# A deformable convolution's sampling loop on one core: a second PSUM buffer for transposed pixels, earlier stores, and other places for scratch data

## The chip, the core and the metric

The kernel runs on one core of a Trainium2 chip. A core has five engines that run side by side and wait for each other on semaphores: TensorE (PE, matrix products, whose results go to PSUM, eight banks[...]), VectorE (DVE), ScalarE (ACT), GpSimd (POOL) and SyncE (SP), which here only issues DMA transfers. The metric is the time of one execution on the device, in microseconds (us). The program's names, which the profile uses, tell which buffer an instruction writes and reads: `pq<-s,xt` is written from `s` and `xt`.

## What is computed

Eight images of 128 channels and 64 x 64 pixels go through two layers. The first is group normalisation, then a deformable 3 x 3 convolution, batch normalisation, ReLU and the residual sum. The second is group normalisation and a mixture of two of four 3 x 3 convolutions with a shared one. The change concerns the deformable convolution:

```python
om = conv(x, off_w) + off_b                       # 3 x 3, 27 channels of offsets and masks
off = om[:, :18].reshape(B, 9, 2, H, W)
mask = sigmoid(om[:, 18:])
py = off[:, :, 0] + (row - 1) + ky                # where each of 9 taps samples, for each pixel
px = off[:, :, 1] + (column - 1) + kx
# val: x at (py, px), bilinear between four pixels, 0 outside the image
val = val * mask
y = einsum('bckhw,ock->bohw', val, w) + b
```

## The kernel before

Bilinear weights are written as "tents": the weight of pixel row r for a sample at py is relu(1 - |py - r|). For each image five tents in y (times the mask) and five in x are made from the offsets, stored to two tables in DRAM, and loaded again, spread over partitions, as `y_wts` and `x_wts`. An image is 11 bands of 6 rows; a band is 11 tiles of 6 x 6 pixels. For each tile VectorE multiplies x and y weights into `s`, TensorE multiplies `s` with the tile's transposed pixels `xt` into `pq`, and ScalarE copies `pq` into `samples`. A band later TensorE convolves the samples into `py`, and ScalarE copies `py` into `y`. The tables of the next image are made beside the bands of this one, in small steps (a `yield` ends a step; `pause(n)` is n of them). The pools and buffers:

```python
ps_s = ctx.enter_context(tc.tile_pool(name="ps_s", bufs=1, space=PSUM))   # for the whole kernel
...                                                                        # in dense(), the first layer:
ps_c = st.enter_context(tc.tile_pool(name="ps_c", bufs=2, space=PSUM))
ps_q = st.enter_context(tc.tile_pool(name="ps_q", bufs=3, space=PSUM))
ps_y = st.enter_context(tc.tile_pool(name="ps_y", bufs=1, space=PSUM))
ps_t = st.enter_context(tc.tile_pool(name="ps_t", bufs=1, space=PSUM))
...
combos = [a1.tile([P, H // 2, W], F32, name=f"combo{i}") for i in range(2)]
tent_y = combos[0].rearrange("p h w -> p (h w)")[0:WB, 0:YSTEP]            # YSTEP is 594
x_wts = [a1.tile([P, NT1, T, T, TAPS], F32, name=f"xwts{i}") for i in range(3)]
y_wts = [a1.tile([P, T, 3, WB, 3], F32, name=f"ywts{i}") for i in range(2)]
samples = [a1.tile([P, T + 2, 3, 3, WB], F32, name=f"samples{i}") for i in range(2)]
```

A pool with n `bufs` hands out n buffers in turn: the instruction that writes the n+1st tile waits until the first has been read. The transposes of a band's pixels, four or three tiles to one PSUM buffer:

```python
def pixels(g):
    xts[g] = a2.tile([P, NT1, P], F32, name="xt")
    for c0 in range(0, NT1, 4):
        n = min(4, NT1 - c0)
        pt = ps_t.tile([P, 4, P], F32, name="pt")
        for c in range(n):
            nc.tensor.transpose(pt[0:QQ, c], picked[g % 2][:, c0 + c]..., ident)
            if c % 2 or c == n - 1:
                yield
        nc.scalar.copy(xts[g][0:QQ, c0 : c0 + n], pt[0:QQ, 0:n])
        yield
        yield
```

The loop over bands issues, for tile c of band g, in this order:

```python
weights(n + AHEAD)                       # VectorE: s, three tiles ahead
sample(n)                                # PE: pq; ScalarE: samples <- pq
load_x(g + 2, ...) or load_y(g + 2, ...) # GpSimd issues the weights of the band after next
next(ended, None)                        # ScalarE: y <- py of the band before, then its statistics and store
if g and c > 1:
    conv(g - 1, c - 2, py)               # PE: py, nine products per band
next(turned, None)                       # PE: transposes of band g + 1; ScalarE: xt <- pt
next(made, None)                         # a step of the next image's tables (normalising, offsets, tents)
if c == 5: pick(g + 2)                   # ScalarE: gathers pixels
```

The tents. For images after the first, each in one of two buffers, stored one step after the next was made:

```python
for i in range(NR):                      # NR is 5
    distance_x(i, every)                 # ScalarE: work[1][i % 2] = |offset + step|
    yield from distance_y(i)             # VectorE
    tent_x(i, every)                     # ScalarE: relu(1 - work)
    yield
    tent_y_of(i)                         # VectorE: work[0][i % 2]
    if i:
        store_y(i - 1)
        store_x(i - 1)
    yield from pause(2)
store_y(NR - 1)
store_x(NR - 1)
```

For the first image nothing runs beside the tables yet. Its y tents lie in the memory of `samples[0]` and its x tents in that of `samples[1]`; the x tents of the first three bands are made early, the rest late:

```python
early, rest = slice(0, FIRST * T), slice(FIRST * T, WB)
for i in range(NR):
    distance_x(i, early); tent_x(i, early)            # ScalarE, in samples[1]
for i in range(NR):
    ... y tents on VectorE, store_y(i); after i == 1 the early x tents are stored; then loads of band 0
pick(0); pixels(0)
for i in range(2):
    distance_x(i, rest); tent_x(i, rest)              # ScalarE, in samples[1]
for r in range(T):
    load_y(0, r, nc.gpsimd if r < 4 else nc.scalar)
pick(1)
for i in range(2, NR):
    distance_x(i, rest); tent_x(i, rest)
for t in (x_wts[1], x_wts[2], y_wts[1]):
    nc.vector.memset(t, 0.0)
for r in range(T):
    load_y(1, r, nc.gpsimd)
for q in range(Q):
    load_x(1, q, nc.sync)
for i in range(NR):
    nc.sync.dma_start(out=<table of x>, in_=<late x tents i>)
```

Of the kernel before, what the change touches and what calls it, by code (L numbers as in the profile page):

```python
# [8 lines left out]
F32 = mybir.dt.float32  # L9
# [7 lines left out]
P = 128  # L17
# [40 lines left out]
def deform_moe_conv(  # L58
# [23 lines left out]
    dram = ctx.enter_context(tc.tile_pool(name="dram", bufs=1, space=DRAM))  # L82
    ps_s = ctx.enter_context(tc.tile_pool(name="ps_s", bufs=1, space=PSUM))

# [27 lines left out]

    def group_affine(stats, scale=None, shift=None):

        mv = small.tile([P, 2], F32, name="mv")
        nc.vector.bn_aggr(mv, stats)
        pm = ps_s.tile([P, 4], F32, name="pm", tag="pss")
        nc.tensor.matmul(pm[:, 0:1], lhsT=gsel, rhs=mv[:, 0:1], start=True, stop=True)
        d = small.tile([P, 1], F32, name="d")
        nc.vector.tensor_tensor(d, mv[:, 0:1], pm[:, 0:1], ALU.subtract)  # L120
        e = small.tile([P, 1], F32, name="e")
        nc.vector.scalar_tensor_tensor(e, d, d, mv[:, 1:2], ALU.mult, ALU.add)
        pv = ps_s.tile([P, 4], F32, name="pv", tag="pss")
        nc.tensor.matmul(pv[:, 0:1], lhsT=gsel, rhs=e, start=True, stop=True)

        gm = small.tile([P, 1], F32, name="gm")
        nc.vector.tensor_tensor(gm, mv[:, 0:1], d, ALU.subtract)
        if scale is None:
            scale = small.tile([P, 1], F32, name="scale")
            shift = small.tile([P, 1], F32, name="shift")  # L130
        rsqrt(scale, pv[:, 0:1], GN_EPS)
        nc.vector.scalar_tensor_tensor(shift, gm, -1.0, scale, ALU.mult, ALU.mult)
        pooled = small.tile([P, 1], F32, name="pooled")
        nc.vector.tensor_tensor(pooled, d, scale, ALU.mult)
        return scale, shift, pooled
# [33 lines left out]
    def dense():  # L169

        with ExitStack() as st:
# [7 lines left out]
            ps_y = st.enter_context(tc.tile_pool(name="ps_y", bufs=1, space=PSUM))  # L179
            ps_t = st.enter_context(tc.tile_pool(name="ps_t", bufs=1, space=PSUM))  # L180

# [59 lines left out]
            def tables(b):  # L241
# [4 lines left out]
                def pause(n):  # L246
                    for _ in range(n):
                        yield
# [23 lines left out]
                yield from pause(3)  # L272
                pm = ps_s.tile([P, 4], F32, name="pm", tag="pss")
                nc.tensor.matmul(pm[:, 0:1], lhsT=gsel, rhs=mv[:, 0:1], start=True, stop=True)
# [7 lines left out]
                yield from pause(2)  # L282
                pv = ps_s.tile([P, 4], F32, name="pv", tag="pss")
                nc.tensor.matmul(pv[:, 0:1], lhsT=gsel, rhs=ev, start=True, stop=True)
# [49 lines left out]
                def tap(j, kx):  # L334

                    if kx == 1:
                        pcs[j] = ps_c.tile([P, CH], F32, name="pc")
                    lo, hi = max(0, 1 - kx), min(W, W + 1 - kx)
                    for q in range(4):
                        nc.tensor.matmul(  # L340
                            pcs[j][32 * q : 32 * q + 32].rearrange("p (h w) -> p h w", w=W)[
                                :, :, lo:hi
                            ],
                            lhsT=weight_of[j][:, kx],
                            rhs=combo_of[j][:, 8 * q : 8 * q + 8, lo + kx - 1 : hi + kx - 1],
                            start=(kx == 1), stop=(kx == 2),
                            skip_group_check=True,
                        )
# [45 lines left out]
                for j in range(4):  # L394
# [9 lines left out]
                    most[:, b : b + 1], omr, AX.X, ALU.max, apply_absolute_value=True  # L404
                )
                yield from pause(9)
                for k in range(3):
# [21 lines left out]
                if b:  # L429
                    work = a1.tile([WB, 2, 2, YSTEP], F32, name="work", tag="om")  # L430
                    tents = [[work[:, a, i % 2] for i in range(NR)] for a in range(2)]
                else:
                    tents = []
                    for t in samples:
                        flat = t.rearrange("p r y x w -> p (r y x w)")
                        tents.append(
                            [flat[0:WB, i * YSTEP : (i + 1) * YSTEP] for i in range(NR)]
                        )
                one = off_x[:, ROWPAD:]
# [26 lines left out]

                def distance_x(i, bases):
                    nc.scalar.activation(
                        tents[1][i].rearrange("p (w y x) -> p x y w", y=3, x=3)[..., bases],
                        by_bases[..., bases], AF.Abs, bias=steps[0:WB, i : i + 1],  # L470
                    )

                def tent_x(i, bases):
                    one = tents[1][i][:, TAPS * bases.start : TAPS * bases.stop]
                    nc.scalar.activation(one, one, AF.Relu, bias=1.0, scale=-1.0)
# [20 lines left out]
                if b:  # L496
                    every = slice(0, WB)
                    for i in range(NR):
                        distance_x(i, every)
                        yield from distance_y(i)  # L500
                        tent_x(i, every)
                        yield
                        tent_y_of(i)
                        if i:
                            store_y(i - 1)
                            store_x(i - 1)
                        yield from pause(2)
                    store_y(NR - 1)
                    store_x(NR - 1)
                    return  # L510
# [3 lines left out]
                for i in range(NR):  # L514
                    distance_x(i, early)
                    tent_x(i, early)
                for i in range(NR):
# [4 lines left out]
                    if i == 1:  # L522
                        for n in range(FIRST):
                            one = tents[1][0][:, n * XSTEP : n * XSTEP + 1]
                            nc.sync.dma_start(
                                out=bass.AP(
                                    tensor=x_table[b].tensor,
                                    offset=x_table[b].offset + (n * NR + NR - 1) * XSTEP,
                                    ap=[[HROW, WB], [HROW - XSTEP, NR], [1, XSTEP]],
                                ),  # L530
                                in_=bass.AP(
                                    tensor=one.tensor, offset=one.offset,
                                    ap=[list(one.ap[0]), [YSTEP, NR], [1, XSTEP]],
                                ),
                            )
# [8 lines left out]
                for i in range(2):  # L544
                    distance_x(i, rest)
                    tent_x(i, rest)
                for r in range(T):
                    load_y(0, r, nc.gpsimd if r < 4 else nc.scalar)
                pick(1)
                for i in range(2, NR):  # L550
                    distance_x(i, rest)
                    tent_x(i, rest)

                for t in (x_wts[1], x_wts[2], y_wts[1]):
                    nc.vector.memset(t, 0.0)
                for r in range(T):
# [3 lines left out]
                for i in range(NR):  # L560
# [6 lines left out]
                        ),  # L567
                        in_=tents[1][i][:, FIRST * XSTEP :].rearrange("p (n k) -> p n k", k=XSTEP),
                    )
# [162 lines left out]
            def reach():  # L732

                near = a1.tile([P, B], F32, name="near")
                nc.vector.tensor_scalar(near, most, float(REACH), None, ALU.is_lt)
                pn = ps_s.tile([P, B], F32, name="pn", tag="pss")
                nc.tensor.matmul(pn[0:1], lhsT=ones_r, rhs=near, start=True, stop=True)
# [77 lines left out]
    def general():  # L815

        with ExitStack() as st:
# [3 lines left out]
            ap4 = st.enter_context(tc.tile_pool(name="ap4", bufs=4))  # L821
            gdram = st.enter_context(tc.tile_pool(name="gdram", bufs=1, space=DRAM))
            ps_o = st.enter_context(tc.tile_pool(name="ps_o", bufs=1, space=PSUM))
            ps_x = st.enter_context(tc.tile_pool(name="ps_x", bufs=1, space=PSUM))
# [57 lines left out]
            def prepare(b, made):  # L882
# [6 lines left out]
                for c in range(NCH):  # L889
                    nc.vector.bn_stats(stats[:, c, :], pad[:, 1 + 8 * c : 9 + 8 * c, 1 : W + 1])  # L890
                scale, shift, _ = group_affine(stats)
                for c in range(NCH):
# [137 lines left out]
    def layer1():  # L1030
# [6 lines left out]
        with ExitStack() as st:  # L1037
            st.enter_context(tc.manual_schedule())
            b1 = st.enter_context(tc.tile_pool(name="b1", bufs=1))
            b2 = st.enter_context(tc.tile_pool(name="b2", bufs=2))  # L1040
            ps_m = st.enter_context(tc.tile_pool(name="ps_m", bufs=7, space=PSUM))
            NG = 4
# [320 lines left out]
```

## Time and profile before

| | |
|---|---|
| time, median of 3 runs | 1690.58 us (1688.41 to 1694.52) |
| span of the profiled execution | 1692.0 us |
| granted TensorE clock, mean | 0.972 of full speed |
| PE busy | 1580.2 us (93%) |
| DVE busy | 1094.8 us (65%) |
| ACT busy | 906.6 us (54%) |
| POOL busy | 955.5 us (56%) |
| moved by DMA | 235.83 MB, mean 139 GB/s |
| first product of a band (`pq`) starts | 68.29 us |
| last copy of `py` to `y` starts | 1306.48 us |

A busy share is an average over stages that have different limits. So the table is read together with the page's 40 slices and with tables by stage: a wait is worth what it costs in its own stage, on the engine that is full there. A matmul here is recorded as two passes, so "x2" of a product is one matmul; the ends of matmuls are modelled, and the starts are the better measure. A wait for several semaphores is put down to the one that came last by the profile.

### The profile page before, as it was taken

The page shows a single profiled execution, that of the slowest core. Times are in us where ns is not written, and L with a number is a line of the kernel's source. Part 1 is how long each engine was busy: PE and PEld are TensorE (multiplying, and loading weights), DVE is VectorE, ACT ScalarE, POOL GpSimd, SP SyncE. Part 2 cuts the span into 40 slices and gives each one's busy share as a digit, 9 for nine tenths or more (in the row PEclk, how much of TensorE's full clock was granted, in tenths as well). Part 3 has the DMA queues.
Part 4 walks back from the last instruction along what each step waited for, and adds up shares of the span by engine and source line. Part 5 has one row for each costly group of instructions (what it writes and reads, how often), then busy time and mean ns, then how long its engine had stood idle before and what let it go on. Part 6 is the DMA issues. An engine that isn't in the chain of part 4 may idle for free. (4 is left out here: it accounts for less than half of the span.)

```text
span 1692.0 us, 21036 instructions
## 1 busy us (share of the span) xinstructions
PE 1580.2 (93%) x6106; PEld 918.2 (54%) x6106; DVE 1094.8 (65%) x2151; ACT 906.6 (54%) x2096; POOL 955.5 (56%) x1518
## 2 busy tenths in 40 slices
PE   3399999999999999999999999999998479999998
PEld 1265665666566556656665665566665234444443
DVE  5755666567575746665665667465443888888882
ACT  2555764766576557647665765576654423333320
POOL 3375685669567666856685676677761412222210
PEclk9589999999999999999999999999999789999999
DMA  4644874776477467647754775665761624443211
GB/s 134 134 120 109 173 173 106 148 181 140 110 164 179 112 130 182 159 104 151 189 132 108 164 184 119 133 161 139 176 147 49 268 95 152 155 153 147 82 58 56
DMA packets 195671, 235.83 MB, mean 139 GB/s; under 512 B 131766, under 2 KB 146098, under 8 KB 195550
## 3 DMA queue, kind: packets, MB, share of 16 engines
q0 software_dynamic: 94768, 124.63, 33.6%
q1 hardware_dynamic: 100047, 109.38, 21.8%
q8 instruction: 54, 0.88, 0.2%
q14 instruction: 68, 0.55, 0.1%
q10 hardware_dynamic: 734, 0.39, 0.1%
HBM read 183.00 MB, written 50.82 MB: 138 GB/s over the span
## 5 line engine op out<-in xcount | busy, mean ns | idle before, releaser
L667 PE MATMUL pq<-s,xt 100*128 100x324 f32 (+2 forms) x1936 | 676.9, 431 | 16.2 <-DVE s L646 14.2
L682 ACT COPY samples<-pq 128x324 f32<-128x324 f32 (+5 forms) x1144 | 429.5, 398 | 462.4 <-PE pq L667 445.8
L646 DVE TENSOR_TENSOR s<-xwts,ywts 100x324 f32<-100x324 f32 x968 | 453.3, 491 | 320.4 <-PE pq L667 298.0
L693 PE MATMUL py<-samples,dw_sb 128*128 128x384 f32 (+1 forms) x1584 | 629.1, 479 | 0.8 <-ACT y L704 0.7
L592 POOL DMA_DIRECT2D xwts<-tabx x862 | 540.7, 635 | 96.0 <-DMA ywts<-taby 37.2
L576 POOL DMA_DIRECT2D ywts<-taby x526 | 303.4, 589 | 292.9 <-DVE s L646 235.6
L667 PEld LDWEIGHTS pq<-s,xt 100*128 100x128 f32 x1936 | 326.8, 192 | 175.4 <-issue 42.5
L693 PEld LDWEIGHTS py<-samples,dw_sb 128*128 128x128 f32 x1584 | 301.2, 191 | 122.9 <-ACT y L704 4.3
L629 PE MATMUL pt<-ident,picked 128*100 128x128 f32 x968 | 196.2, 278 | 35.1 <-ACT picked L616 19.7
L629 PEld LDWEIGHTS pt<-ident,picked 128*100 128x100 f32 x968 | 117.1, 129 | 177.0 <-issue 67.3
L1277 PE MATMUL pc<-v,u 128*128 128x512 f32 x384 | 172.6, 598 | 9.3 <-DVE u L1226 9.3
L1277 PE MATMUL pc<-v,wmix 128*128 128x512 f32 x384 | 176.1, 604 | 0.0
L636 ACT COPY xt<-pt 100x512 f32<-100x512 f32 (+1 forms) x264 | 147.0, 557 | 3.2 <-PE pt L629 3.2
L707 DVE BATCH_NORM_STATS2 ystats<-y 128x6 f32<-128x384 f32 (+1 forms) x88 | 48.2, 548 | 139.5 <-ACT y L704 139.5
L1277 PEld LDWEIGHTS pc<-v,u 128*128 128x128 f32 x384 | 72.6, 191 | 98.2 <-issue 85.0
L1277 PEld LDWEIGHTS pc<-v,wmix 128*128 128x128 f32 x384 | 72.3, 191 | 88.3 <-issue 84.7
L1255 ACT ACTIVATE t<-pc,bmix 128x512 f32<-128x512 f32 x32 | 22.0, 687 | 182.3 <-PE pc L1277 100.3
L1105 POOL TENSOR_TENSOR x<-x,xt 128x512 f32<-128x512 f32 x32 | 47.2, 1507 | 85.1 <-ACT x L1103 85.1
L608 ACT COPY picked<-pad 128x900 f32<-128x900 f32 x88 | 91.3, 1037 | 2.0 <-DMA xwts<-tabx 2.0
L323 DVE TENSOR_TENSOR combo<-pad 128x1024 f32<-128x1024 f32 x64 | 77.0, 1220 | 17.7 <-PE pc L340 10.1
L1105 POOL TENSOR_TENSOR pad<-pad,pad 128x512 f32<-128x512 f32 x28 | 39.6, 1441 | 71.7 <-ACT pad L1103 71.5
L783 DVE COPY samples<-samples 128x1188 f32<-128x1188 f32 x80 | 61.4, 767 | 0.0
(148 smaller groups left out, 1036.7 us busy)
## 6 DMA issues: line engine op xcount, KB each, us to landing
ywts<-taby POOLq DMA_DIRECT2D x526, 116.0 KB, 4.2
pad<-in_x_dram SPq DMA_DIRECT2D x48, 512.0 KB
xwts<-tabx POOLq DMA_DIRECT2D x172, 116.0 KB, 4.0
out_dram<-yo SPq DMA_DIRECT2D x32, 512.0 KB
xwts<-tabx POOLq DMA_DIRECT2D x173, 92.8 KB, 3.8
yd<-y SPq DMA_DIRECT2D x80, 192.0 KB
xwts<-tabx POOLq DMA_DIRECT2D x172, 69.6 KB, 3.6
pad<-yd SPq DMA_DIRECT2D x16, 512.0 KB
```

The source lines that it names most:

```text
L323: nc.vector.tensor_tensor(combo_of[j][:, half * n : half * n + n], *rows, op)
L576: engine.dma_start(out=y_wts[g % 2][r * Q : (r + NR) * Q, r].rearrange("p a b c -> p (a b c)"), in_=bass.AP(tensor=y_table[b].tensor, offs ...
L592: engine.dma_start(out=x_wts[g % 3][q:QQ:Q, :, lo:hi].rearrange("p t a b c -> p t (a b c)"), in_=bass.AP(tensor=x_table[b].tensor, offset= ...
L608: nc.scalar.copy(picked[g % 2][:, 1 : NT1 - 1], bass.AP(tensor=one.tensor, offset=one.offset, ap=[list(one.ap[0]), [T, NT1 - 2], [W, Q], [ ...
L629: nc.tensor.transpose(pt[0:QQ, c], picked[g % 2][:, c0 + c].rearrange("p y x -> p (y x)"), ident,)
L636: nc.scalar.copy(xts[g][0:QQ, c0 : c0 + n], pt[0:QQ, 0:n])
L646: nc.vector.tensor_tensor(s[0:QQ], x_wts[g % 3][0:QQ, c].rearrange("p a r (y x) -> p (r y) a x", x=3), y_wts[g % 2].rearrange("p r y a x - ...
L667: nc.tensor.matmul(pq[asked], lhsT=xts[g][0:QQ, c], rhs=ss.pop(n)[0:QQ].rearrange("p m a x -> p m (a x)")[asked], start=True, stop=True,)
L682: nc.scalar.copy(rows[:, 6 + m0 : 6 + m1, x, T * c + lo : T * c + hi], by_columns[:, m0:m1, x, lo:hi],)
L693: nc.tensor.matmul(py[:, first:], lhsT=dw_sb[:, 3 * ky + kx], rhs=samples[g % 2][:, first + ky : T + ky, 2 - ky, 2 - kx, kx : kx + W], sta ...
L1105: adder.tensor_tensor(y, y, xt[:, c * CH : (c + 1) * CH], ALU.add)
L1277: nc.tensor.matmul(pc, lhsT=us[j][:, kx], rhs=vs[g][:, rows, kx : kx + W], start=(kx == 0), stop=(kx == 2),)
```

## The change

It has four parts.

1. **Two PSUM buffers for transposed pixels.** `ps_t` gets a second buffer in the first layer. All eight banks were in use, so the bank of `ps_s` is given up there: the small products of the group statistics use the `pc` buffers of the offset convolution instead, and `ps_s` is opened anew in the later parts. It is for PE to transpose the next group while ScalarE has not yet copied the last.
2. **Tents stored as soon as made** (images after the first): `store_x(i)` and `store_y(i)` follow tent i at once, so that a tent's buffer comes free earlier.
3. **The first image's x tents out of the samples' memory**: the early ones into the free part of `combos[0]`, four of the late ones into `om`, whose content has been stored by then, and the fifth into `combos[0]`. It is for band 1's samples not to wait until those tents are stored.
4. **Memsets**: that of `x_wts[2]` moves to an earlier place on VectorE, and that of `y_wts[1]` goes to GpSimd.

The number of instructions of PE and ScalarE and their order do not change. VectorE has one fewer and GpSimd one more. SyncE issues the tents' stores in another order. The diff, cut to its core:

```diff
-    ps_s = ctx.enter_context(tc.tile_pool(name="ps_s", bufs=1, space=PSUM))
...
-            ps_t = st.enter_context(tc.tile_pool(name="ps_t", bufs=1, space=PSUM))
+            ps_t = st.enter_context(tc.tile_pool(name="ps_t", bufs=2, space=PSUM))
...
-                pm = ps_s.tile([P, 4], F32, name="pm", tag="pss")
+                pm = ps_c.tile([P, CH], F32, name="pm", tag="pc")
...                                       # the same for pv and pn
+                if b == 0:
+                    nc.vector.memset(x_wts[2], 0.0)      # after the offsets' maximum
                 yield from pause(9)
...
-                    for t in samples:
-                        flat = t.rearrange("p r y x w -> p (r y x w)")
-                        tents.append([flat[0:WB, i * YSTEP : (i + 1) * YSTEP] for i in range(NR)])
+                    one = samples[0].rearrange("p r y x w -> p (r y x w)")[0:WB]
+                    tents = [[one[:, i * YSTEP : (i + 1) * YSTEP] for i in range(NR)]]
+                    one = combos[0].rearrange("p h w -> p (h w)")[0:WB, YSTEP:]
+                    n = FIRST * XSTEP
+                    early_x = one[:, 0 : NR * n].rearrange("p (i n) -> p i n", i=NR)
+                    late = [om.rearrange("p a n -> p (a n)")[0:WB], one[:, NR * n :]]
+                    n = YSTEP - n
+                    late_x = [late[i // 4][:, i % 4 * n : (i % 4 + 1) * n] for i in range(NR)]
...
                         tent_y_of(i)
-                        if i:
-                            store_y(i - 1)
-                            store_x(i - 1)
-                        yield from pause(2)
-                    store_y(NR - 1)
-                    store_x(NR - 1)
+                        store_x(i)
+                        yield
+                        store_y(i)
+                        yield
...
-                for t in (x_wts[1], x_wts[2], y_wts[1]):
-                    nc.vector.memset(t, 0.0)
+                nc.vector.memset(x_wts[1], 0.0)
+
+                nc.gpsimd.memset(y_wts[1], 0.0)
                 for r in range(T):
                     load_y(1, r, nc.gpsimd)
...                                       # in the later parts of the kernel:
+            ps_s = st.enter_context(tc.tile_pool(name="ps_s", bufs=1, space=PSUM))
```

## What was predicted, before the changed kernel had run

> **What bounds the kernel now.** I read the page's slices first, then the table by stage, then the waits, and only then the timeline at the places that the waits named. Slices (each digit is a tenth of busy time in 1/40 of the span, 42.3 us):
>
> ```profile
> PE   3399999999999999999999999999998479999998
> ...
> PEclk9589999999999999999999999999999789999999
> ```
>
> TensorE is full except in the first two slices and near slice 32. Table by stage (stretch in us, its length, then busy time of PE, PEld, DVE, ACT, POOL, the granted clock, DMA share, GB/s):
>
> ```profile
> 0.00:68.30 68.30, 19.05 (x112) 8.18 (x112) 42.62 (x62) 25.69 (x58) 19.47 (x53) 0.76 0.46 125
> 68.30:90.00 21.70, 16.71 (x51) 11.46 (x52) 13.46 (x29) 8.63 (x25) 15.89 (x27) 0.66 0.85 165
> 290.00:1250.00 960.00, 948.31 (x4054) 589.99 (x4047) 585.06 (x1208) 607.72 (x1478) 670.24 (x1106) 1.00 0.65 148
> 1360.00:1692.00 332.00, 322.87 (x774) 143.99 (x774) 258.39 (x469) 96.12 (x141) 70.38 (x55) 0.98 0.30 114
> ```
>
> There are four stages. Up to 68.3 us the first image's tables are made. From 68.3 to 90 the bands start, with the DMA engines at 0.85 and the clock at 0.66. From there to about 1307 come the 88 bands, where PE is busy 948 of 960 us: **this stage is PE's, and the change can win at most its bubbles.** The last 380 us are the second layer, which the change touches only by renaming a PSUM buffer. Waits from 140 to 1310 us (total us, times, longest):
>
> ```profile
> PE pt L629 <- ACT xt L636: 13.1, 26, 1.2
> ...
> ACT work L468 <- DMA tabx<-work: 3.8, 8, 0.6
> ...
> PE py L693 <- ACT y L704: 0.7, 1, 0.7
> ```
>
> The only real PE wait in the bands is the one that the first part of the change aims at: 13.1 us, about four times per image. In a full band the pixel transposes come as four, four, three; with one buffer each group waits until ScalarE has copied the group before it out. One of those places, at a band's end (start us, duration, engine, line, what; then idle before it and its releaser):
>
> ```profile
> 500.22 1.39 ACT L468 ACTIVATE work<-combo,steps 66x594 f32<-66x594 f32 x1
> 500.69 0.65 PE L667 MATMUL pq<-s,xt 100*128 100x288 f32 x2
> 501.81 0.48 ACT L636 COPY xt<-pt 100x384 f32<-100x384 f32 x1
> 502.34 0.42 PE L629 MATMUL pt<-ident,picked 128*100 128x128 f32 x2 [1.00 <-ACT xt L636]
> 503.12 0.60 ACT L704 ACTIVATE y<-py,db_sb 128x384 f32<-128x384 f32 x1
> 503.92 0.49 PE L693 MATMUL py<-samples,dw_sb 128*128 128x384 f32 x1
> ```
>
> See that ScalarE is late because it makes the next image's tents (1.39 us each) between copies, and that right after the transposes PE needs something else from the same late ScalarE: the copy of `y` out of the single `py` buffer. And the start of the bands:
>
> ```profile
> 63.84 3.03 DVE L555 MEMSET ywts<- 128x3564 f32 x1 [0.69 <-DMA xwts<-tabx]
> 67.16 3.40 POOL L576 DMA_DIRECT2D ywts<-taby  x6 [4.62 <-DVE ywts L555]
> 67.74 2.53 DVE L646 TENSOR_TENSOR s<-xwts,ywts 100x324 f32<-100x324 f32 x6 [0.88 <-DMA xwts<-tabx]
> ...
> 80.12 0.50 DVE L646 TENSOR_TENSOR s<-xwts,ywts 100x324 f32<-100x324 f32 x1 [3.14 <-DMA tabx<-samples]
> ...
> 82.28 1.43 PE L667 MATMUL pq<-s,xt 100*128 100x324 f32 x2
> ...
> 87.79 1.15 ACT L682 COPY samples<-pq 128x270 f32<-128x270 f32 x4 [8.28 <-DMA tabx<-samples]
> 88.33 0.50 PEld L667 LDWEIGHTS pq<-s,xt 100*128 100x128 f32 x2 [2.13 <-ACT samples L682]
> ...
> 94.64 0.71 PE L667 MATMUL pq<-s,xt 100*128 100x324 f32 x2
> ```
>
> **What the Trainium skill says.** (1) "Perfetto Trace Analysis", Optimizing Tensor Performance, Matmuls: independent groups should rotate through PSUM banks so that the evacuation of one overlaps the matmuls of the next. The 13.1 us agree. (2) "TensorE: Matmul & The Clock Gate", What's actually happening: PE's clock is halved after an idle window and released by sustained work. Agrees: two records of a 324-column product take 1.43 us at 82.28 and 0.71 at 94.64, so an idle time near 80 us costs more than itself. (3) "VectorE: DVE Perf Modes", Zero memsets: one cycle per element, so 3564 elements at the page's 0.96 GHz give an estimate of 3.71 us. The row says 3.03, but the three memsets start at 56.40, 60.12 and 63.84, 3.72 apart: the pitch agrees. (4) "SBUF — State Buffer", Who interferes with whom: a VectorE instruction of this kind does not hold up GpSimd. Agrees: the four y loads that GpSimd issued at 60.27 beside a memset took 0.57 us each, as elsewhere (median 0.577).
>
> **The change part by part.**
>
> *x tents out of `samples`.* The first image's x tents lie in the memory of the second band's samples. Their five late stores are issued from 72.92 for 8.35 us, so ScalarE's first copy of band 1 sits idle 8.28 us, until 87.79. PE runs ahead by the three `pq` buffers, then stands. Band 1's products start at 80.76, 82.28, 83.92, then 88.33 (tile 3), 90.42 (4), 92.78 (5), 94.64 (6). Without the wait tile 3 follows about 1.6 us after tile 2 at the halved clock, near 85.7; the clock comes up after some 5 us of work (as it did between 68.3 and 73.5), so tiles 4 to 6 follow at the 1.2 us pitch of the later tiles: tile 6 near 89.4. **Saved: 94.6 - 89.4 = 5.2 us.** PE is full from there on, so all of it reaches the end.
>
> *Memsets.* The one of `x_wts[2]` goes to 34.6 us, when VectorE is idle (its next work starts at 43.77). The one of `y_wts[1]` goes to GpSimd, which is free from 62.55 (the last y load of band 0 starts at 61.98 and takes 0.57) to 67.16; at the 3.07 us that GpSimd took for the same size at 4.40 us it ends near 65.7, so band 1's y loads start some 1.2 us sooner. The first weights at 67.74 gain almost nothing: the last y load of band 0 starts at 61.98 and takes 5.4 us to land, 67.4, and 63.84 + 3.72 = 67.56 was a tie with it. Band 1's weights (80.12) wait for both y and x loads, and the x loads do not move; with DMA at 0.85 I count 0.5 us of the 1.2. **Saved: 0.5 us.**
>
> *Two `pt` buffers.* Starts of PE's instructions give the true bubbles beside one image's tables: 0.58 us at 406.8, 0.37 at 410.1, 0.59 at 487.6, 1.17 at 501.2; 2.71 in all, more than the listed waits because ends are modelled. The first two come from normalising the next image's pixels on ScalarE, the other two from its tents. With a second buffer PE goes on, but then `py` must be free. At 410: PE starts the convolution at 412.09 and, 0.95 ahead, would start it at 411.14, but the `y` copy ends at 411.21; so 0.88 of 0.95 stays. At 501: PE would start the convolution 1.76 earlier than 503.92, at 502.16, but `y` ends at 503.72. ScalarE has no gap from 492.7 on, so `y` is where it is, **and the one microsecond becomes a wait for `py`.**
>
> *Tents stored at once.* ScalarE's wait of 0.46 us at 492.70 (3.8 us in all, in the list above) was for the store of the tent two steps back, which the old order issued one step late. It goes, and since ScalarE is then behind until the band ends, `y` comes 0.46 earlier, 503.26: PE starts at 503.26 in place of 503.92. So the tents give 0.66 per image, the normalising 0.88; **together 1.5 us for each of the 7 images made beside the bands: 10.5 us.**
>
> *PSUM renames.* The two statistics products per image take `pc` buffers, which are read out long before they are needed again: 0.
>
> Sum: 5.2 + 0.5 + 10.5 = 16.2; I take off 1 for loads that now meet more traffic at the start. 1690.6 - 15.2 = **1675.4, say 1675 us.**
>
> **Rivals.** *A: the bubbles only change their name.* ScalarE could be the bound of the tent bands, and `py <- y` (0.7 us in 1170 now) would take all of it. For it: ScalarE without a gap in those bands. Against it: the page's 54% for ScalarE over the span. Then only the start wins: about 1685. *B: the loads bind the start.* With ScalarE free, PE would reach band 2 near 94 and find its weights late. For it: DMA at 0.85 until 90, and 3.14 us of waiting for band 1's loads. Against: band 2's last y loads are issued by 85.6 and land about 4.5 us later, at 90. It would cost 2 to 3 us: 1678. *C: GpSimd's memset holds up the loads* that share its queue, moving the first product by up to 3 us: again 1678. *D: all bubbles go*, 2.71 x 7 = 19 us, and PE's clock stays up at 80 us: about 1665.
>
> **Range and chances.** D is the floor and A the ceiling, and both are unlikely in full; the times before spread over 6 us. I set 1667 to 1684. For 2% (33.8 us) there aren't enough bubbles: even D gives 25. Faster by over 2%: 0.02; within 2%: 0.96; slower: 0.02.
>
> **What would show it.** In the changed kernel's waits `pt <- xt` is near zero, and `py <- y` has grown to 3 to 7 us; `work <- tabx` is gone. ScalarE's copies of band 1 start within a microsecond of their products, and the 1.4 us pairs of half-clock products end near 86 rather than 94. The first `y` copy, at 101.09 now, comes near 95.5. The second layer takes as long as before. I am wrong if `pt <- xt` stays, if a wait for weights appears between 80 and 110 us, or if a stage after 1310 moves.

## Result, and the profile after

| | before | after |
|---|---|---|
| time, median (lowest to highest), 4 runs each | 1691.83 us (1688.41 to 1694.52) | 1677.87 us (1675.21 to 1679.23) |
| ratio, 95% interval | | 0.9917, [0.9893, 0.9940] |
| first copy of `py` to `y` (start of the bands) | 101.09 us | 96.36 us |
| from the first to the last copy of `py` to `y` (88 bands) | 1205.39 us | 1196.93 us |
| from there to the last output of the second layer | 378.59 us | 377.30 us |

The change wins 14.0 us, 0.8%. The last three rows are from the two traces: 4.7 us at the start, 8.5 us in the bands, and 1.3 us in the second layer, where the change should have done nothing. Slices of the page of the changed kernel:

```profile
PE   3399999999999999999999999999998489999998
...
PEclk9599999999999999999999999999999689999999
```

PE's row is as full as before. In the row of the clock the third slice (84 to 126 us) has gone from 8 to 9; the other digit that differs in each row is at the change of the layers, where slices of a shorter span cut the stages elsewhere. The table by stage of the changed kernel (stretch, length, then busy time of PE, PEld, DVE, ACT, POOL, the granted clock, DMA share, GB/s):

```profile
68.30:90.00 21.70, 17.82 (x64) 12.25 (x64) 14.64 (x33) 10.01 (x28) 14.80 (x26) 0.74 0.77 163
290.00:1240.00 950.00, 944.22 (x4035) 594.17 (x4034) 582.81 (x1207) 605.29 (x1477) 668.08 (x1104) 1.00 0.65 149
```

In the first 21.7 us of the bands PE has 64 records of matmuls where it had 51, at a clock of 0.74 in place of 0.66. In the bands proper PE's idle share has fallen from 1.22% (11.69 of 960 us) to 0.61% (5.78 of 950). Waits of PE from 140 to 1300 us in the changed kernel (total us, times, longest):

```profile
PE py L689 <- ACT y L700: 6.0, 7, 1.0
```

One line is left. The wait for a transpose buffer (`pt`, 13.1 us) has gone, and seven waits for `y` are there. Six of them (5.3 us) stand in its place, at the end of the tents of six of the seven images made beside the bands. The seventh, 0.7 us in the last band, the kernel before had too. The timeline of the changed kernel at one of them (start us, duration, engine, line, what; idle before it and its releaser) is the same place that the prediction showed at 502 us:

```profile
493.37 0.52 ACT L678 COPY samples<-pq 128x270 f32<-128x270 f32 x2
...
493.78 0.46 ACT L632 COPY xt<-pt 100x384 f32<-100x384 f32 x1
...
494.15 0.69 ACT L477 ACTIVATE work<-work 66x594 f32<-66x594 f32 x1
494.75 0.46 ACT L678 COPY samples<-pq 128x270 f32<-128x270 f32 x2
...
495.09 0.58 ACT L700 ACTIVATE y<-py,db_sb 128x384 f32<-128x384 f32 x1
...
495.72 0.59 PE L689 MATMUL py<-samples,dw_sb 128*128 128x384 f32 x1 [0.96 <-ACT y L700]
```

See that ScalarE goes from one instruction straight to the next, and the copy of `y` has its turn only at 495.09. PE has finished its transposes and stands 0.96 us until the copy has ended. Now the start of band 1 in the changed kernel:

```profile
80.55 0.50 DVE L642 TENSOR_TENSOR s<-xwts,ywts 100x324 f32<-100x324 f32 x1 [4.09 <-DMA xwts<-tabx]
...
81.19 1.30 PE L663 MATMUL pq<-s,xt 100*128 100x288 f32 x2 [3.74 <-DVE s L642]
...
82.53 0.49 ACT L678 COPY samples<-pq 128x270 f32<-128x270 f32 x2 [4.22 <-PE pq L663]
...
84.42 1.29 PE L663 MATMUL pq<-s,xt 100*128 100x324 f32 x2
...
86.44 0.79 PE L663 MATMUL pq<-s,xt 100*128 100x324 f32 x2
...
89.91 0.71 PE L663 MATMUL pq<-s,xt 100*128 100x324 f32 x2
```

ScalarE's first copy of the band starts at 82.53, just after the first product, and no longer at 87.79. PE goes on without standing still, and after three pairs of products at half clock (1.3 to 1.4 us) the clock is up: from 86.44 on a pair takes 0.7 to 0.8 us. Tile 6 starts at 89.91, before at 94.64. But the first weights of the band (80.55) are no earlier than before (80.12). Since band 0 ended 1.2 us sooner, PE's wait for them has even grown, from 2.10 to 3.74 us.

### The profile page after: what moved, and what is told of

The parts are those of the page before. It is cut to its first block, busy times and chain, and to the rows that moved or that the text cites. A ratio compares the mean times of both kernels' runs of the same rounds, so it can differ in the third digit from the quotient of the medians.

```text
span 1677.5 us, 20746 instructions
## 1 busy us (share of the span) xinstructions
PE 1575.5 (94%) x6106; PEld 922.9 (55%) x6106; DVE 1089.8 (65%) x2150; ACT 903.9 (54%) x2096; POOL 956.1 (57%) x1519
## 5 line engine op out<-in xcount | busy, mean ns | idle before, releaser
L625 PEld LDWEIGHTS pt<-ident,picked 128*100 128x100 f32 x968 | 124.3, 129 | 146.2 <-issue 67.4
```

What stands on the lines that cost most here:

```text
L625: nc.tensor.transpose(pt[0:QQ, c], picked[g % 2][:, c0 + c].rearrange("p y x -> p (y x)"), ident,)
```

## The experiments

Two questions were open: which part of the change gives which gain, and whether the remaining wait for `y` comes of the single `py` buffer or of ScalarE's backlog. Ratios are to the kernel before, run on the same chip beside each experiment, with 95% intervals. "Start" is the first copy of `py` to `y`, "bands" the time from it to the last one.

**Each part alone**, put on the kernel before:

```diff
 # e1_two_pt
-            ps_t = ...tile_pool(name="ps_t", bufs=1, space=PSUM)
+            ps_t = ...tile_pool(name="ps_t", bufs=2, space=PSUM)   # ps_s given up for it, pm, pv, pn in pc
 # e2_stores
                         tent_y_of(i)
-                        if i: store_y(i - 1); store_x(i - 1)
-                        yield from pause(2)
-                    store_y(NR - 1); store_x(NR - 1)
+                        store_x(i)
+                        yield
+                        store_y(i)
+                        yield
 # e3_xtents: the first image's x tents in combos[0] and om, as the change has them; one pt buffer
 # e4_memsets
-                for t in (x_wts[1], x_wts[2], y_wts[1]): nc.vector.memset(t, 0.0)
+                nc.vector.memset(x_wts[1], 0.0)       # x_wts[2] earlier, where the change has it
+                nc.gpsimd.memset(y_wts[1], 0.0)
```

Expected of the second `pt` buffer: 

> Only the second buffer for transposed pixels (with the statistics in the pc buffers), on the kernel before. Theory: it takes away the waits of the transposes (13.1 us) in full, but at the end of the tent bands a wait for py takes their place, and it is longer than the 6.0 us of the changed kernel, because ScalarE still waits 0.46 us per image for the store of a tent: 8 to 10 us of waits for py. The 87 bands from the first to the last copy of y, 1205.4 us before and 1196.9 in the changed kernel, take 1199 to 1201. The first y copy stays near 101. Time about 5.5 us below the kernel before. Rival (bubbles only change their name): waits for py of 12 us or more and bands within 1.5 us of 1205.4. Rival (all bubbles go): bands near 1193 and no wait for py.

Expected of the stores: 

> Only the tents stored as soon as made, on the kernel before. Theory: ScalarE no longer waits 0.46 us per image for a store, and because it is behind until the end of the tent bands, the copies there come 0.46 us earlier: the transposes' waits fall from 13.1 to about 10 us, the bands from 1205.4 to about 1202.5 us, the time by about 3 us. Rival: ScalarE has slack and the store order is worth nothing alone: bands within 0.7 us of 1205.4.

Expected of the x tents: 

> Only the first image's x tents out of the samples' memory (the statistics in pc buffers, but one buffer for transposed pixels), on the kernel before. Theory: the whole gain of the start is this: the first y copy comes at 96 to 97 us in place of 101.1, bands stay at 1205.4, time about 4.7 us below before. Rival (loads bind the start): PE finds the weights of band 1 or 2 late, and the first y copy comes at 99 us or later.

Expected of the memsets: 

> Only the two memsets moved, on the kernel before. What the prediction counted: 0.5 us, first y copy at 100.6. What the changed kernel's trace suggests instead: GpSimd starts the loads of band 1's y weights and of band 2 about 1.8 us sooner, these share the DMA engines with band 1's x loads, and band 1 starts no sooner than at 80.8 (81.2 in the changed kernel): first y copy at 101.1 to 101.6, time within 1 us of before.

| | time (before beside it 1694.26) | ratio | start | bands |
|---|---|---|---|---|
| second `pt` buffer | 1686.03 | 0.9954 [0.9937, 0.9970] | 101.36 | 1201.11 |
| stores | 1686.66 | 0.9961 [0.9950, 0.9972] | 96.47 | 1203.39 |
| x tents | 1688.20 | 0.9968 [0.9957, 0.9978] | 96.33 | 1206.40 |
| memsets | 1692.13 | 0.9998 [0.9983, 1.0014] | 98.89 | 1208.69 |

Three parts gain and the memsets do not. The stores' start of 96.47 was not expected: in that kernel the x tents still lie in the samples' memory, and ScalarE still waited 7.7 us for them. The memsets' start of 98.89 was not expected either (101.1 to 101.6). So two kernels were each run once more, unchanged: the kernel before, and the stores alone.

Expected of the kernel before: 

> The kernel before, a second trace. The first y copy came at 101.1, 101.4, 98.9 and 96.5 us in the four kernels that keep the first image's x tents in the samples' memory, and at 95.7 to 96.4 in the five that do not. Theory: ScalarE's wait is there each time (6.5 to 8.9 us), but what it costs depends on whether TensorE's clock has come up before PE stands still: here again anything from 96.5 to 101.5, with the half-clock products (1.3 to 1.45 us a pair) after the wait if it is late. If it is 101.1 again, the kernel before has a fixed start. Bands 1205 to 1209 us.

Expected of the stores: 

> The kernel with the store order alone, a second trace. Its time fell by 6.6 us where its bands gave 2.0 to 3.4, and its first y copy came at 96.5. If that start was chance, the first y copy now comes anywhere up to 101.5; if the store order really helps the start (nothing in it runs before the first y copy of the second image's tables), it is 96.5 again. Bands 1202.5 to 1204.5.

The kernel before took 1690.59 us and started its bands at 100.40, the stores took 1687.16 (one run each, 1691.34 for the kernel before beside them) and started at 100.99. The early start of the stores' first trace was chance. (Bands took 1204.39 and 1200.61 us, both shorter than expected.) The two traces of the stores show what differs. PE's and ScalarE's timeline in the first:

```profile
83.39 1.29 PE L665 MATMUL pq<-s,xt 100*128 100x324 f32 x2
84.47 0.85 PE L691 MATMUL py<-samples,dw_sb 128*128 128x256 f32 x2
85.16 0.28 PE L274 MATMUL pm<-mv,gsel 128*128 128x1 f32 x2
85.99 1.15 ACT L680 COPY samples<-pq 128x270 f32<-128x270 f32 x4 [7.71 <-DMA tabx<-samples]
86.53 0.81 PE L665 MATMUL pq<-s,xt 100*128 100x324 f32 x2 [1.09 <-ACT samples L680]
87.62 0.71 PE L665 MATMUL pq<-s,xt 100*128 100x324 f32 x2
```

and in the second:

```profile
83.26 0.84 PE L665 MATMUL pq<-s,xt 100*128 100x324 f32 x2
...
87.91 1.15 ACT L680 COPY samples<-pq 128x270 f32<-128x270 f32 x4 [8.80 <-DMA tabx<-samples]
88.45 1.45 PE L665 MATMUL pq<-s,xt 100*128 100x324 f32 x2 [3.80 <-ACT samples L680]
90.55 1.29 PE L665 MATMUL pq<-s,xt 100*128 100x324 f32 x2
```

ScalarE was released at 85.99 us in the first and at 87.91 in the second: 1.9 of the 4.5 us between their starts are tents' stores that landed later. The rest goes with the clock. Here is the granted clock (the number after the busy times) over stretches of the first trace, then of the second:

```profile
78.20:84.95 6.75, 4.73 (x12) 3.11 (x13) 5.37 (x12) 0.08 (x1) 4.90 (x8) 0.50 0.97 174
85.00:90.00 5.00, 3.90 (x20) 3.00 (x19) 2.98 (x9) 2.83 (x9) 4.57 (x9) 1.00 0.61 149
```

```profile
80.15:83.50 3.35, 3.35 (x9) 2.19 (x10) 3.35 (x8) 0.00 (x0) 1.86 (x4) 0.50 0.94 167
83.55:86.90 3.35, 1.11 (x6) 0.80 (x5) 2.52 (x6) 0.00 (x0) 2.59 (x5) 1.00 0.95 177
86.95:93.75 6.80, 5.30 (x12) 3.79 (x13) 1.35 (x5) 2.50 (x7) 4.66 (x8) 0.50 0.51 114
```

In both the clock had fallen in the wait for band 1's weights or just as it ended. In the first it was up again at 85, before PE stood for ScalarE, and a stand of 1.09 us did not bring it down (0.81 us a pair after it). In the second it was up sooner, at 83.5, but PE then stood 3.80 us, the clock fell once more, and the products after it were slow (1.45) until 93.8. In the kernel before the stand for ScalarE (2.05 us, in its repeat 0.98) came while the clock was still down, and it stayed down until 94.1 and 93.9.

The Trainium skill ("TensorE: Matmul & The Clock Gate", What's actually happening) says that the clock follows PE's activity in a window that runs freely, so that the place of the change varies from run to run. These two traces of one program agree: the clock first falls at 78.15 us in one and at 80.11 in the other, and its stretches at half speed last 6.8, 3.4 and 6.8 us, whole numbers of steps of 3.4.

With all traces taken together, the start with the x tents in the samples' memory was 101.1, 100.4, 101.4, 98.9, 96.5 and 101.0, mean 99.9. With them elsewhere it was 96.4, 96.3, 95.7, 95.9 and 96.0, mean 96.1 (left out are three kernels below that also change the loads or the number of `pq` buffers). **That part is worth 3.8 us on the mean, between about nothing and 5 in a single run.** An estimate from the same traces gives nearly as much. PE's stand for ScalarE, 0.5 to 3.8 us, is 1.7 on the mean. And PE was at work at half clock for 9.6 us at this place, with the tents elsewhere for 5.6; half of the difference, 2.0 us, is lost to the clock.

The bands can be taken apart in the same way. Below is the pitch of the copies of `y`, added over the seven images that have tables made beside them, in us. The tents are made in the sixth and seventh of an image's eleven pitches.

| | normalising and other bands | tent bands | 77 bands |
|---|---|---|---|
| as before (before, its repeat, x tents alone, memsets alone; mean) | 891.5 | 193.3 (191.4 to 195.7) | 1084.8 |
| second `pt` buffer alone | 886.3 | 193.7 | 1080.0 |
| stores alone (mean of two) | 891.3 | 189.3 (188.0, 190.6) | 1080.5 |
| the change (mean of four, with variants below that leave the bands alone) | 886.4 | 188.8 (188.2 to 189.5) | 1075.2 |

**The second buffer wins 5.2 us, and none of it in the tent bands; the stores win 4.0 us, and all of it there.** The two add up to 9.2, beside 9.6 for the whole. The other bands agree within 0.4 us among the four traces of the first row; the tent bands scatter by 4.3, as much as the stores win, but all six traces with the new order (188.0 to 190.6) lie below all five with the old (191.4 to 195.7). With the second buffer alone PE's waits for `pt` were gone and those for `y` were 6.9 us in 8 places, where the kernel before had only the 0.7 us of the last band; 1.3 us for `pq` were new. In the tent bands the wait had only moved.

**The change again, and with the memsets back on VectorE.**

```diff
 # e5_after_old_memsets, on the changed kernel
-                if b == 0: nc.vector.memset(x_wts[2], 0.0)
...
-                nc.vector.memset(x_wts[1], 0.0)
-                nc.gpsimd.memset(y_wts[1], 0.0)
+                for t in (x_wts[1], x_wts[2], y_wts[1]): nc.vector.memset(t, 0.0)
```

Expected of the changed kernel: 

> The changed kernel once more, on the chip of the next three, to have them side by side. Theory: its gain comes from two places, the start (first y copy at 96 to 97 us) and the bands (1196.9 us in the first trace); if the 1.3 us by which the second layer was shorter in the first trace is chance, it is between 374 and 379 us here and not always below 378.6.

Expected of the old memsets: 

> The changed kernel with the three memsets back on VectorE. The prediction's 0.5 us would show as a time 0.5 us longer and a first y copy 0.5 us later than in the changed kernel. Theory now: band 1 starts when band 1's x loads land, which the memsets do not move, so nothing changes: first y copy between 96.0 and 97.0, time within 1.5 us of the changed kernel.

The changed kernel took 1676.31 us (ratio 0.9918 [0.9902, 0.9935]; before beside it 1691.55), with the old memsets 1677.46 (0.9919 [0.9906, 0.9932]). They started their bands at 95.71 and 95.88. No gain of the memsets shows, alone or in the whole; the intervals would not show 0.5 us, but band 1's first weights were ready at 80.55 and 79.70 in the two traces with the change's memsets and at 79.55 with the old ones. Why does an earlier issue not bring band 1 earlier? With the change GpSimd issues band 1's y loads at 65.37 in place of 67.16, but it then goes on at once to band 2's x loads, at 68.86, while band 1's are still under way. So those were held back:

```diff
 # e7_late_x2, on the changed kernel
-                if b == 0: nc.vector.memset(x_wts[2], 0.0)
...
                 for r in range(T): load_y(1, r, nc.gpsimd)
+                nc.gpsimd.memset(x_wts[2], 0.0)          # band 2's x loads wait for it
```

Expected: 

> The changed kernel with x_wts[2] cleared by GpSimd after it has issued band 1's y loads, which holds back the loads of band 2's x weights by 3 us. Theory: band 1's weights are late because band 2's loads share the DMA engines with them; they now land 1 to 2 us sooner (first weights of band 1 at 78.5 to 79.5 in place of 80.55), PE's 3.74 us wait shrinks as much, and the first y copy comes at 94.5 to 95.5. Rival: band 1's own x loads, which SyncE issues until 73, set the time whatever runs beside them: first weights of band 1 still at 80 to 81, and band 2's loads, 3 us later, make a new wait near 94.

The time was 1671.81 us, ratio 0.9891 [0.9877, 0.9904]: 4.5 us less than the changed kernel beside it, with equal bands (1196.19 and 1196.30). GpSimd in this kernel:

```profile
65.84 3.39 POOL L571 DMA_DIRECT2D ywts<-taby  x6 [0.30 <-POOL ywts L549]
69.18 3.12 POOL L552 MEMSET xwts<- 128x3564 f32 x1
72.60 3.55 POOL L587 DMA_DIRECT2D xwts<-tabx  x6 [0.29 <-POOL xwts L552]
```

and the start of band 1 there:

```profile
78.00 0.49 DVE L641 TENSOR_TENSOR s<-xwts,ywts 100x324 f32<-100x324 f32 x1 [1.45 <-DMA xwts<-tabx]
...
78.64 0.72 PE L662 MATMUL pq<-s,xt 100*128 100x288 f32 x2 [1.10 <-DVE s L641]
```

Band 2's loads start 3.7 us later (72.60), and band 1's first weights are ready 2.5 us sooner (78.00 in place of 80.55). PE stands 1.10 us in place of 3.74, and the clock does not come down at all: the first pair takes 0.72 us. The bands start at 92.58, earlier than the theory had it (94.5 to 95.5); in a kernel below that keeps this edit they start at 91.32, again without a fall of the clock.

**The wait for `y`.** Is it the single buffer, its place in the order, or ScalarE's backlog?

```diff
 # e6_y_first, on the changed kernel: y copied ahead of the band's first tile
+                    if c == 0: next(ended, None)
                     sample(n)
...
-                    next(ended, None)
+                    if c: next(ended, None)
 # e8_py2_pq2, on the changed kernel: eight banks, one taken from pq
-            ps_q = ...bufs=3        ps_y = ...bufs=1
+            ps_q = ...bufs=2        ps_y = ...bufs=2
 # e9_x_tents_dve, on e7_late_x2: the last step of later images' x tents from ScalarE to VectorE
-        nc.scalar.activation(one, one, AF.Relu, bias=1.0, scale=-1.0)
+        nc.vector.tensor_scalar(one, one, 1.0, 0.0, ALU.subtract, ALU.min)   # minus the tent; the y tents
+                                                                             # are negated too
```

Expected of `y` first: 

> The changed kernel with ScalarE's copy of py to y issued ahead of the copy of the new band's first samples, not after it. Theory: the 6.0 us of waits for py at the ends of the tent bands are ScalarE's backlog, and the y copy now comes 0.45 us sooner per image: waits for py fall to 2 to 3.5 us, bands from about 1197 to about 1194 us, time 3 us below the changed kernel. Rival: the samples' copy is then late and PE waits for a pq buffer instead: bands stay at 1197, and waits of pq for samples appear.

Expected of two `py` and two `pq`: 

> The changed kernel with a second py buffer, paid for with the third pq buffer. It asks whether the 6 us of waits for py are a matter of that one buffer or of ScalarE's backlog. Theory (backlog): waits for py go to zero, but PE meets ScalarE at the next buffer: waits of pq for the samples' copies appear, of 6 us or more, and the bands take as long as in the changed kernel (1196.3 to 1196.9) or longer. Rival (the buffer): bands about 1190 us, no new wait.

Expected of tents on VectorE: 

> The kernel with x_wts[2] cleared late (the fastest so far: bands 1196.2 us, first y copy 92.6), and of each later image's x tent the second step (relu, 0.7 us on ScalarE, five per image) on VectorE instead, as min(w - 1, 0), with the y tents negated as well so that the product is the same. Theory (backlog of ScalarE): with 3.5 us less on ScalarE in the tent bands the y copy comes in time, the waits for py fall from 5.9 us to below 1.5, the tent bands from about 14.1 to 13.3 us, the bands to 1190 to 1191 us. Rival: VectorE, nearly full in those bands, is then late with the weights: a wait of pq for s appears and the bands do not get shorter.

With `y` first the time was 1677.66 us (0.9914 [0.9897, 0.9931]), the bands 1195.81: no gain that shows beside the changed kernel. PE's waits from 140 to 1280 us, without the last band (in the first trace of the changed kernel 5.3 us in 6 places, for `y` alone):

```profile
PE py L689 <- ACT y L700: 3.1, 6, 0.6
PE pq L663 <- ACT samples L678: 1.2, 3, 0.6
```

Part of the wait has moved to the copy that had to give way. With two `py` buffers it was 1683.82 us (0.9972 [0.9962, 0.9982]), the bands 1203.51, and

```profile
PE pq L663 <- ACT samples L678: 8.3, 13, 0.9
```

The wait for `py` is gone, but the tent bands are no shorter for it: 188.9 in the table's measure, 188.8 in the change. Of the waits for `pq`, seven (3.0 us) are in the tent bands and six (5.3 us) at the turn of an image, in its eleventh pitch, which takes 86.3 us over the seven images in place of 80.8: that is the price of the `pq` buffer given up. A second `py` buffer beside three for `pq` was not tested. So neither the other order nor this exchange of buffers gains time. The third kernel takes 0.7 us of work per tent off ScalarE: 1668.54 us (0.9882 [0.9862, 0.9901]), the bands 1191.72, tent bands 185.1 in the table's measure. Of PE's waits for `y` the one of 0.7 us in the last band is left, and none at the tents. One tent stretch of the changed kernel by the table by stage, and the same stretch (8 us earlier) with tents on VectorE:

```profile
484.00:496.00 12.00, 11.04 (x45) 6.97 (x44) 10.77 (x29) 11.80 (x26) 6.73 (x12) 1.00 0.66 156
```

```profile
476.00:488.00 12.00, 12.00 (x49) 7.75 (x48) 12.00 (x30) 10.76 (x24) 5.36 (x9) 1.00 0.56 147
```

ScalarE was busy 11.80 of 12 us and PE 11.04; with ScalarE at 10.76 PE is full. VectorE is now full in its place (12.00), so moving more work there promises nothing; that was not tried. This is the fastest kernel of the study: 20.7 us under the kernel before, beside which it ran. Against the version that only holds back band 2's loads (0.9891), the timed ratios do not separate it; its trace has 4.5 us less in the bands.

## Why the prediction was right

1675 us was predicted, 1677.87 measured. By its own steps:

- **Two `pt` buffers, 0.88 per image: right in kind, a little large.** The buffer's gain lies outside the tent bands, as predicted: 5.1 us of the whole change in seven images, 0.73 each. At the turn of the image (first and last pitch), where the 0.88 had been read off, it is 0.49; the rest is spread over the other bands, which the prediction had not counted. In the tent bands the buffer won nothing by itself, since the wait went over to `py`: 6.0 us, within the 3 to 7 given.
- **Tent bands, 0.66 per image: right.** The tent bands of the change are 4.5 us shorter in seven images, 0.64 each; the stores alone give 4.0, more than their share of 0.46 per image (3.2). But the sign named for it, that `work <- tabx` would be gone, failed: 2.5 us of it is left in the change (3.8 before). Over all traces with these tents on ScalarE it is 2.6 to 6.0 us with the old order and at most 2.5 with the new: the wait shrinks, but some stores still land after their buffer is wanted.
- **x tents out of `samples`, 5.2 us: right in the pair of traces that it was read from, too large on the mean.** Tile 6 went from 94.64 to 89.91, predicted 89.4, and the start of the bands from 101.09 to 96.36. Over all traces it is 3.8. The mis-sized term is what the wait costs: the prediction took one trace's stand of PE and its half-clock products as fixed. Over six traces the stand was 0.5 to 3.8 us, and the clock stayed down for none to two steps of 3.4 us longer than without the wait. In the stores' first trace, where the clock was up before PE stood and the tents' stores landed first of all, ScalarE's wait of 7.7 us cost next to nothing.
- **Memsets, 0.5 us: wrong; no gain shows** (0.9998 alone). The sum counted y loads issued 1.2 us sooner; they came 1.8 sooner, and the weights of band 1 no sooner. That the loads bind this place was the thought of rival B, which put it one band too late: band 2's loads were in time, and it was band 1's weights that came late because of them. The run that held them back showed it. By the letter, one sign of being wrong (a wait for weights between 80 and 110 us) was there, at 81.19; but the kernel before has this wait too, at 80.76, and no other was added.
- **PSUM renames, 0: as predicted** as far as the bands show. The second layer was 1.3 us shorter in the first pair of traces. In the other traces, in which its code is the same, it took from 374.2 to 378.9 us, with or without the renames, so this is scatter.
- **The 1 us taken off for traffic** finds nothing that answers to it: the first product of band 1 started at 80.8 and 80.7 us in the two traces of the kernel before, at 81.2 and 80.3 in those of the changed one.

The sum in the place of the predicted 15.2 is 3.8 + 9.6 = 13.4 us, and the times say 14.0. That 1675 came so near is in part luck: the terms for the start, the bands and the memsets were 1.4, 0.9 and 0.5 us too large, and the 1 us for traffic, which answers to nothing, took a third of that back. The range was built on rivals A and D. A, that all bubbles only change their name, came true for the one bubble per image at the tents' end, and of D the part that PE's clock stays up came true only when band 2's loads were held back as well.

Two things stay open. The three gaining parts alone were timed, by their ratios, at 7.8, 6.6 and 5.4 us, 19.8 together (each within 2 to 3 us), which is more than the 14 of the whole (10 to 18). They add up in the traces' bands, and the start is in part chance. The kernel before took 1694.26 us beside these runs and 1689.24 to 1691.83 beside the others; whether that is the reason isn't known. And that it was DMA bandwidth that band 2's loads took, rather than a place in a queue, was not tested: only that their later issue brought band 1's weights sooner.

## What to carry to other kernels

When PE waits for a buffer, look at the next thing that PE needs from the same engine: if that engine has no gap there, a further buffer only renames the wait, and the gain comes from taking work or waits off that engine. A pitch of one repeated instruction, added up by place in the loop, tells parts of a change apart where times of the whole scatter by several microseconds (here within 0.4 us over seven images, except in the tent bands). At a start that is full of transfers, what is issued for later can delay what is needed now; holding it back for 3 us was worth more than issuing the early loads sooner.

## What the runs showed of the hardware that was not expected

The cost of a stand of PE is not proportional to its length; it depends on where it falls. With the clock up, stands of 1.10 us (band 2's loads held back) and 1.09 us (the stores' first trace) left it up: 0.72 and 0.81 us a pair after them. A stand of 3.80 us (the stores' second trace) brought it down for 6.8 us. In the wait for band 1's weights less was enough: the clock fell in or just after stands of 1.84 to 2.10 us in four traces (the kernel before twice, the memsets alone, the stores' second). So the idle window that the prediction names need not be a whole step of 3.4 us. With the clock already down, even short stands were followed by more slow products: 0.98 us in the repeat of the kernel before by three pairs (1.45, 1.28, 1.28), 0.48 us with the memsets alone by two (1.45, 1.28).
